# Layer 0's written order at the turn of a period: first taps, position weights, transposes and output sums

## The chip, the cores and the metric

The kernel runs on one core of one Trainium2 chip. The metric is the device time of one execution in microseconds. The core's engines are named as in the profile: PE (TensorE), with its weight loads PEld; DVE (VectorE); ACT (ScalarE); POOL (GpSimd); SP (SyncE, which here issues DMAs). Each engine works through its own list of instructions, and semaphores order the lists among each other.

## The reference, cut to what matters

The input x has the shape (2, 512, 64, 64). Two layers follow each other, each added to its input. Layer 0 is a deformable convolution on a group norm of x; layer 1 is an attention with batch norm, and the change doesn't touch it. Of layer 0:

```python
xproj = inp @ in_w + in_b                        # inp: x, normalised, channels last
x1 = depthwise_conv_3x3(x, dw_w) + dw_b
x1 = layernorm_over_channels(x1) * ln_g + ln_b
x1 = gelu(x1)
offset = x1 @ off_w + off_b                      # 16 groups, 9 points, 2 coordinates
mask = softmax((x1 @ mask_w + mask_b).reshape(N, H, W, 16, 9), -1)
out = sum over the 9 points of mask * bilinear(xproj at base + offset)
out = out @ out_w + out_b
x = x + out
```

The kernel's fast path reads the offsets as smaller than one pixel: then every output pixel is a weighted sum over a 5 x 5 window of xproj, with weights that follow from offsets and mask.

## The kernel before

Layer 0 is cut into 16 chunks (NSEQ), 8 rows of one image each. Four stages work on a chunk. Each is a Python generator whose `yield` ends a step:

- `project` (L724): three loads of raw rows; four ACT activations that write xn, the normalised rows (L748); then four times the projection pq on PE (L758), its copy xj on ACT (L764), and two stores to the padded image xt in HBM (L766).
- `features` (L771): one step of four ACT activations, the first tap of the depthwise convolution for each of four blocks of channels (L783); 32 taps on DVE (L788), eight a block, where POOL adds the blocks up (`tot`, L794 and L796); the mean over channels on PE (p_mean, L801); the subtraction (L806) and squares (L809); the variance, its root on ACT (L818) and reciprocal on DVE (L820, L821); two steps of GELU on ACT (L825).
- `weights` (L833): four times a matmul group po (L842) and its sum o (L847); exp, the one-dimensional weights and the softmax's sum; nine steps (pk, L885, and aw, L890) that sum products into aw, the 25 position weights of a pixel; one ACT copy `at` (L893) that reorders them; and four steps of four transposes p_tr on PE (L901) with a copy awT on ACT (L902).
- `sample` (L919): eight steps that spread the weights (pb on PE, L930, copied to bt by ACT, L935); eight steps, in two halves s of four blocks cb, that multiply patches of xt with bt (pa, L949, 8 products, each in two passes) and copy the result to dT on ACT (L960, four copies); in the second half each also loads the residual `res` (L941), and the last step of each half loads the next chunk's patches (`fetch`, L914, eight DMAs). Then four times the output projection py (L969) and a step with its sum (L974), statistics (L975) and store (L976), called t0 to t3 here.

The main loop runs under `tc.manual_schedule()`: each engine does its instructions in the order in which Python wrote them. That order is `period` (L998). Period i calls steps of several chunks in turn: `y`, the output half of `sample(i-1)`; `v`, the last four steps (the transposes) of `weights(i)`; `m`, `sample(i)`; `w`, `weights(i+1)`; `f`, `features(i+2)` from its DVE taps on; `g`, the first step of `features(i+3)`; `p`, `project(i+3)`; and `more`, one piece of the second image's statistics (loads xraw, L711, and bn_stats, L713), which last through periods 0 to 4. `m`, `w` and `g` are handed on as `y`, `v` and `f` of the next period. "The turn" is where one period ends and the next begins.

At the turn, the order before is, by engine (numbers count the blocks of a stage):

- PE: pa12, pq2, pa13, pq3, py0, transposes 0 to 3, pb0, pb1, po0. (pa12 is half 1, block 2.)
- ACT: GELU, xj1, dT12, xj2, dT13, first taps, xj3, `at`, awT0 to awT3, bt0, bt1.
- DVE: pk7, pk8, four taps, t0 and its statistics, nine taps, o0, seven taps, o1, and so on.
- SP: stores of xj2, load of res3, eight patch loads, stores of xj3, one xraw, three raw loads, store of t0.

In PSUM, tiles of tag "mm" (pq, py, p_tr, po, p_mean and the group norm's) share four buffers in rotation, tiles of tag "big" (pb, pa) two.

Of the kernel before, what the change touches and what calls it, by code (L numbers as in the profile page):

```python
# [570 lines left out]
def window_path(ctx: ExitStack, tc: tile.TileContext, t_in: dict, out: bass.AP, far: bass.AP, sums: bass.AP):  # L571
# [58 lines left out]
    with ExitStack() as l0:  # L630
# [66 lines left out]
        def image_stats(n):  # L697

            mv = sm.tile([P, KB, 2], F32, name="gn_mv")
            size = CH if n == 0 else CH // 2  # L700
            pieces, ahead = deque((kb, h) for kb in range(KB) for h in range(S // size)), deque()
            for kb in range(KB):
                st = sm.tile([P, 16, 6], F32, name="gn_st")
                for h in range(S // size):
                    if n == 0:
                        t = img[kb][:, h * size : (h + 1) * size]
                    else:
                        while len(ahead) < 3 and pieces:
                            k2, h2 = pieces.popleft()
                            ahead.append(io.tile([P, size], F32, name="xraw", bufs=3))  # L710
                            nc.sync.dma_start(ahead[-1], x_v[n, :, k2, h2 * size : (h2 + 1) * size])  # L711
                        t = ahead.popleft()
                    nc.vector.bn_stats(st[:, h, :], t)  # L713
                    yield
                nc.vector.bn_aggr(mv[:, kb, :], st[:, : S // size].rearrange("p a b -> p (a b)"))
            yield
            result = []
            yield from group_norm_steps(mv, KB, sm, ps, result)
            sc, bi = result
            gn[n] = [sm.tile([P, KB], F32, name=f"gn_{k}{n}") for k in ("scale", "bias")]  # L720
            nc.vector.tensor_copy(gn[n][0], sc)
            nc.vector.tensor_copy(gn[n][1], bi)
# [184 lines left out]
        def fetch(i, s):  # L907

            if i >= NSEQ:
                return  # L910
            n, ch = divmod(i, NCH)
            t = io.tile([P, PX, C], F32, name="patch", bufs=2)
            for p in range(PX):
                nc.sync.dma_start(  # L914
                    t[:SN, p, :], xt_d[n][ch * ROWS + PR * s : ch * ROWS + PR * s + SY, PC * p : PC * p + SX, :]
                )
            patches[i, s] = t

        def sample(i):  # L919

            n, ch = divmod(i, NCH)
            at = [awT[32 * t : 32 * t + NW].rearrange("w g (c s r p) -> w c r g s p", c=2, s=2, r=PR) for t in range(4)]

            for d0 in range(0, PR * PC, 4):
                pb = ps.tile([P, 4, 2 * PX * G], F32, tag="big", bufs=2, name="pb")

                for k in (0, 2, 1, 3):
                    r, c = divmod(d0 + k, PC)
                    off, t = SEL0 - (r * SX + c), c // 2
                    nc.tensor.matmul(  # L930
                        pb[:SN, k, :], sel[32 * t : 32 * t + NW, off : off + SN], at[t][:, c % 2, r], start=True, stop=True
                    )

                copy = nc.vector.tensor_copy if i == NSEQ - 1 and d0 % PC else nc.scalar.copy
                copy(bt[:SN].rearrange("s g q d -> s d (g q)")[:, d0 : d0 + 4, :], pb[:SN])  # L935
                yield
            res = {}

            def read(cb):
                res[cb] = io.tile([P, CH], F32, name="res", bufs=4)  # L940
                nc.sync.dma_start(res[cb], x_v[n, :, cb, ch * CH : (ch + 1) * CH])  # L941

            dT = cv.tile([P, KB, CH], F32, tag="dT", name="dT", bufs=2)
            for s in range(2):
                xp = patches.pop((i, s))
                for cb in range(KB):
                    pa = ps.tile([P, PX, 4, PR * PC], F32, tag="big", bufs=2, name="pa")
                    for p in range(PX):
                        nc.tensor.matmul(  # L949
                            pa[:, p], xp[:SN, p, cb * P : (cb + 1) * P],  # L950
                            bt[:SN, 4 * cb : 4 * cb + 4, PX * s + p, :], start=True, stop=True,
                        )

                    for q in range(4):
                        rows = slice(CG * q, CG * (q + 1))
                        dst = dT[rows, cb, s * (CH // 2) : (s + 1) * (CH // 2)].rearrange(
                            "p (r q c) -> p q r c", r=PR, c=PC)
                        src = pa[rows, :, q, :].rearrange("p q (r c) -> p q r c", c=PC)
                        copy = nc.vector.tensor_copy if i == NSEQ - 1 and q % 2 else nc.scalar.copy
                        copy(dst, src)  # L960
                    if s:
                        read(cb)
                    if cb == KB - 1:
                        fetch(i + 1, s)
                    yield
            for cb in range(KB):
                py = ps.tile([P, CH], F32, tag="mm", name="py")
                for kb in range(KB):
                    nc.tensor.matmul(  # L969
                        py, out_w[:, kb, cb * P : (cb + 1) * P], dT[:, kb, :], start=(kb == 0), stop=(kb == KB - 1)  # L970
                    )
                yield
                t = res.pop(cb)
                nc.vector.scalar_tensor_tensor(t, py, out_b[:, cb : cb + 1], t, ALU.add, ALU.add)  # L974
                nc.vector.bn_stats(stats2[n][:, cb, ch, :], t)  # L975
                nc.sync.dma_start(x1_d[n][ch][:, cb, :], t)  # L976
                yield
# [20 lines left out]
        def period(y, v, m, w, f, g, p, more):  # L998

            p()
            y()
            v(4)
            f(4)
            y()
            for taps in (9, 7, 6, 6):
                m(2)
                w()  # L1010
                more()
                f(taps)
                w()
                more()
            w()
            m()
            w()
            m()
            f()
            y()  # L1020
            f()
            m()
            p()
            w(2)
            y(2)
            w()
            m()
            p()
            f()
            w(2)  # L1030
            p()
            y(2)
            f()
            y()
            m()
            p()
            more()
            for k, steps in enumerate((1, 2, 2, 2)):
                p()
                w(steps)  # L1040
                if k == 0:
                    f()
                p()
                more()
                if k < 3:
                    m()
                if k == 0:
                    f()
                if k == 2:
                    g()  # L1050
            w()

        def value_weights():

# [26 lines left out]
        v = Chain(weights, 0)  # L1081
        v(23)
        run(features(1), project(2), output_bias())
        fetch(0, 0)
        fetch(0, 1)
        later, y, f = image_stats(1), Chain(sample, NSEQ), Chain(features, 2)
        with tc.manual_schedule():
            f()
            for i in range(NSEQ):
                if i == NCH - 3:  # L1090
                    run(later)
                w, m, g = Chain(weights, i + 1), Chain(sample, i), Chain(features, i + 3)
                period(y, v, m, w, f, g, Chain(project, i + 3), lambda: next(later, None))
                y, v, f = m, w, g
            y.rest()
# [5 lines left out]
    with ExitStack() as l1, tc.manual_schedule():  # L1101
# [8 lines left out]
        with ExitStack() as at, ExitStack() as inner:  # L1110
# [177 lines left out]
            for n in range(NB):  # L1288
# [9 lines left out]
                for i in range(NCH // 2):  # L1298
                    if 0 < i < 3 or n and i == 0:
                        k = i + 1 if i else 1  # L1300
# [26 lines left out]
                for qb in range(NCH):  # L1327
                    acc = {}
                    for kp in range(NPAIR + 2):
# [23 lines left out]
                        if kp < NPAIR:  # L1353
                            v = ready.pop(0)
                            e, tt, _ = made[qb, kp]
                            ops = operands(lambda k: e[:, k, :], tt)
                        else:
                            v = w7[:, kp - NPAIR]
# [174 lines left out]
```

## Time and profile before

| What | us |
|---|---|
| median of three runs | 3701.42 (3700.8 to 3702.75) |
| the profiled execution's own time | 3707.44 |
| its span, first to last instruction | 3705.6 |
| of it, layer 0's periods 1 to 5 and the end of 0 (233 to 615) | 382 |
| of it, periods 6 to 12 (615 to 1089) | 474 |
| of it, periods 13 to 15 and the last outputs (1089 to 1276) | 187 |

A period is counted from the first output projection py0. Periods 6 to 12 are 67.7 us each; periods 1 to 5, which also carry statistics of the second image, are 74.0 to 75.9 us; from chunk 13 on there is nothing left to project, and the periods are shorter. All times in microseconds "from the start" are on the clock of this one profiled execution.

In lines of instructions, the columns are start, duration, engine, line, operation, output <- inputs with shapes and the count of instructions merged into the line; in brackets stands how long the engine was idle before, and what ended it. In lines of waits: engine, what waited, <- what it waited for, then the total, the number of waits, and the longest.

### The profile page before, as it was taken

To read this page: it belongs to the slowest core of one execution; us is meant where nothing else is said; L and a number is where in the kernel's file an instruction comes from. 1 tells how busy PE (TensorE), PEld (TensorE's weight loads), DVE (VectorE), ACT (ScalarE), POOL (GpSimd) and SP (SyncE) were. 2 spreads that over 40 slices of the span, in tenths; PEclk is the share of its full clock that TensorE was granted. 3 is DMA by queue.
4 is the path that set the end of the run, shared out by engine and by line. 5 is a ranking of instruction groups with operands and counts; after the bars stand their busy time and mean duration, and the time that the engine had idled before them with its cause. 6 is when DMAs were issued, how large, how long until landed. Compare 5 with 4: busy or idle time off the path is not lost.

```text
span 3705.6 us, 39010 instructions
## 1 busy us (share of the span) xinstructions
PE 3417.9 (92%) x15151; PEld 2433.8 (66%) x15151; DVE 2345.8 (63%) x3575; ACT 1304.1 (35%) x1691; POOL 291.0 (8%) x190
## 2 busy tenths in 40 slices
PE   4689998999998799999999999999999999999990
PEld 1355555555555477777777777777777777777770
DVE  5798989999996475545554554567455455545544
ACT  2476777787886321111111111221111111111114
POOL 2112111212111030000000000022000000000000
PEclk9789999999999899999999999999999999999995
DMA  7233442342432444334334333444433333243349
GB/s 240 63 98 114 135 137 83 115 133 83 127 109 78 142 157 171 126 129 139 123 108 163 122 125 130 140 155 169 149 121 111 122 138 111 101 149 121 111 162 389
DMA packets 180181, 500.06 MB, mean 135 GB/s; under 512 B 22640, under 2 KB 64368, under 8 KB 170512
## 3 DMA queue, kind: packets, MB, share of 16 engines
q1 hardware_dynamic: 176496, 473.34, 37.5%
q10 hardware_dynamic: 3456, 24.12, 1.7%
q8 instruction: 121, 1.98, 0.2%
q14 instruction: 76, 0.62, 0.0%
q0 software_dynamic: 32, 0.00, 0.0%
HBM read 406.09 MB, written 91.29 MB: 134 GB/s over the span
## 4 chain that ended last, share of the span: by engine, by line
PE 75%; DVE 15%; DMA 4%; ACT 2%; SPq 1%; issue 1%; POOL 1%; ACTq 0%; DVEq 0%; POOLq 0%
PE acc L1364 41%; DVE conv L788 8%; PE pS L1211 7%; PE p L1402 7%; PE py L969 5%; PE pq L758 4%; PE pa L949 4%; PE pv L1251 3%; PE pk L1305 1%; PE p_mean L801 1%; DVE pk L885 1%; DVE aw L890 1%; DMA patch<-xt 1%; DMA out<-ct 1%; DVE o L847 1%
## 5 line engine op out<-in xcount | busy, mean ns | idle before, releaser
L1364 PE MATMUL acc<-e,v 128*128 128x256 f32 x3072 | 768.2, 386 | 0.0
L1215 ACT ACTIVATE e<-pS 128x1024 f32<-128x1024 f32 x256 | 262.0, 1024 | 1386.4 <-PE pS L1211 1313.0
L1364 PE MATMUL acc<-tt,v 128*128 128x256 f32 x3072 | 748.2, 380 | 0.5 <-DMA v<-wv 0.5
L1364 PEld LDWEIGHTS acc<-e,v 128*128 128x128 f32 x3072 | 566.5, 190 | 233.2 <-issue 165.3
L1364 PEld LDWEIGHTS acc<-tt,v 128*128 128x128 f32 x3072 | 582.4, 190 | 91.2 <-issue 10.6
L1218 DVE TENSOR_TENSOR t<-e 128x256 f32<-128x256 f32 x256 | 108.8, 425 | 761.1 <-ACT e L1215 761.1
L788 DVE SCALAR_TENSOR_TENSOR conv<-xn,L_conv_dw_w_sb,conv 128x504 f32<-128x504 f32 (+1 forms) x512 | 399.7, 795 | 48.5 <-ACT conv L783 36.5
L1228 DVE TENSOR_TENSOR tot<-tot,e 128x512 f32<-128x512 f32 x480 | 330.1, 688 | 8.3
L949 PEld LDWEIGHTS pa<-bt,patch 96*128 96x128 f32 x2048 | 251.8, 197 | 63.1 <-issue 39.4
L1211 PE MATMUL pS<-q,kq 64*128 64x512 f32 x1024 | 289.0, 641 | 0.0
L949 PE MATMUL pa<-bt,patch 96*128 96x128 f32 x2048 | 255.3, 281 | 9.3 <-ACT dT L960 5.8
L935 ACT COPY bt<-pb 96x1024 f32<-96x1024 f32 x124 | 234.2, 2001 | 58.9 <-PE pb L930 58.9
L758 PE MATMUL pq<-L_conv_in_w_sb,xn 128*128 128x512 f32 x512 | 236.3, 605 | 4.3 <-ACT xn L748 4.3
L969 PE MATMUL py<-dT,L_conv_out_w_sb 128*128 128x512 f32 x512 | 238.0, 610 | 0.0
L1402 PE MATMUL p<-t,v 128*128 128x256 f32 x1024 | 231.4, 382 | 1.7 <-DMA v<-wv 1.7
L1402 PEld LDWEIGHTS p<-t,v 128*128 128x128 f32 x1024 | 192.1, 190 | 48.5 <-issue 21.2
L960 ACT COPY dT<-pa 32x256 f32<-32x256 f32 x496 | 179.5, 362 | 89.8 <-PE pa L949 80.9
L842 PE MATMUL po<-om_w_pg,feat 128*128 128x432 f32 x512 | 203.4, 542 | 0.0
L969 PEld LDWEIGHTS py<-dT,L_conv_out_w_sb 128*128 128x128 f32 x512 | 99.3, 197 | 119.6 <-issue 115.5
L758 PEld LDWEIGHTS pq<-L_conv_in_w_sb,xn 128*128 128x128 f32 x512 | 94.1, 194 | 109.5 <-issue 93.0
L842 PEld LDWEIGHTS po<-om_w_pg,feat 128*128 128x128 f32 x512 | 93.0, 191 | 90.5 <-issue 89.4
L1211 PEld LDWEIGHTS pS<-q,kq 64*128 64x128 f32 x1024 | 77.1, 184 | 84.9 <-issue 84.9
(203 smaller groups left out, 3731.2 us busy)
## 6 DMA issues: line engine op xcount, KB each, us to landing
v<-wv SPq DMA_DIRECT2D x252, 768.0 KB
patch<-xt SPq DMA_DIRECT2D x256, 192.0 KB
v<-wv SPq DMA_DIRECT2D x256, 128.0 KB
wv<-v SPq DMA_DIRECT2D x32, 896.0 KB
xt<-xj SPq DMA_DIRECT2D x128, 128.0 KB
res<-in_x SPq DMA_DIRECT2D x64, 256.0 KB
wx<-res SPq DMA_DIRECT2D x64, 256.0 KB
xq<-wx SPq DMA_DIRECT2D x16, 1024.0 KB
```

The lines of the kernel that those rows point to most:

```text
L758: nc.tensor.matmul(pq, xn[:, kb, 1 + 2 * t : 3 + 2 * t, :].rearrange("p r c -> p (r c)"), in_w[:, kb, :], start=(kb == 0), stop=(kb == KB ...
L788: nc.vector.scalar_tensor_tensor(dst, src, wt, dst, ALU.mult, ALU.add)
L842: nc.tensor.matmul(po[:, : 3 * GP], f[:, kb, t * P : (t + 1) * P], om_w[:, kb].rearrange("p a k g -> p (a k g)"), start=(kb == 0), stop=(k ...
L935: copy(bt[:SN].rearrange("s g q d -> s d (g q)")[:, d0 : d0 + 4, :], pb[:SN])
L949: nc.tensor.matmul(pa[:, p], xp[:SN, p, cb * P : (cb + 1) * P], bt[:SN, 4 * cb : 4 * cb + 4, PX * s + p, :], start=True, stop=True,)
L960: copy(dst, src)
L969: nc.tensor.matmul(py, out_w[:, kb, cb * P : (cb + 1) * P], dT[:, kb, :], start=(kb == 0), stop=(kb == KB - 1))
L1211: nc.tensor.matmul(pS[:, h, :], kq[r, 2 * (kp // 4) + h, c0 : c0 + P], qs[qb][r, :], start=True, stop=True)
L1215: nc.scalar.activation(e.rearrange("p a q -> p (a q)"), pS.rearrange("p h q -> p (h q)"), AF.Exp)
L1228: nc.vector.tensor_add(tots[qb], tots[qb], e2[:, h, :])
L1364: nc.tensor.matmul(acc[j][:, cb * HQ : (cb + 1) * HQ], v[:, j, cb * P : (cb + 1) * P], ops[j], start=(kp + cb == 0), stop=(kp + cb == NPAI ...
L1402: nc.tensor.matmul(p7[:, cb * HQ : (cb + 1) * HQ], v7[:, cb * P : (cb + 1) * P], t3, start=(k + cb == 0), stop=(k + cb == NPAIR + 2),)
```

## The change

`period` is written anew around the turn, and `sample` gets one more `yield`, between the products pa and their copies to dT, so that the two can be called apart. Everywhere but in the last of the eight such steps `m(2)` calls them together, as `m()` did.

By engine, the turn then reads (what moves is in bold):

- PE: pa12, pq2, pa13, pq3, **transposes 0 to 3, py0**, pb0, pb1, po0.
- ACT: GELU, **first taps**, xj1, dT12, xj2, **`at`**, xj3, **dT13**, awT0 to awT3, bt0, bt1.
- DVE: as before: pk7, pk8, four taps, t0 and its statistics, nine taps, o0.
- SP: stores of xj2, **stores of xj3, one xraw**, load of res3, eight patch loads, three raw loads, store of t0.

No instruction is added or taken away.

```diff
@@ sample
                             bt[:SN, 4 * cb : 4 * cb + 4, PX * s + p, :], start=True, stop=True,
                         )
+                    yield
 
                     for q in range(4):
@@ period
             p()
+            v(4)
             y()
-            v(4)
             f(4)
             y()
             for taps in (9, 7, 6, 6):
@@
             w()
-            m()
+            m(2)
             w()
-            m()
+            m(2)
             f()
             y()
             f()
-            m()
+            m(2)
             p()
             w(2)
             y(2)
             w()
-            m()
+            m(2)
             p()
             f()
             w(2)
@@
             y(2)
             f()
             y()
+            m(2)
+            p()
+            more()
+            p()
+            w()
+            f()
+            p()
+            more()
+            m(2)
+            f()
+            p()
+            w(2)
+            g()
+            p()
+            more()
+            m(2)
+            p()
+            w(2)
+            p()
+            more()
             m()
             p()
+            w(3)
+            p()
             more()
-            for k, steps in enumerate((1, 2, 2, 2)):
-                p()
-                w(steps)
-                if k == 0:
-                    f()
-                p()
-                more()
-                if k < 3:
-                    m()
-                if k == 0:
-                    f()
-                if k == 2:
-                    g()
-            w()
+            m()
```

## The prediction

> **What bounds the kernel now.** I read the page first, then a table of busy time by stretches, then the chain of waits inside one stretch, then the waits of single engines there, and last each engine's instructions in order of time around one turn.
>
> The page gives shares of the whole span, which mixes layer 0 (to about 1270 us) with the attention layer:
>
> ```profile
> PE 3417.9 (92%) x15151; PEld 2433.8 (66%) x15151; DVE 2345.8 (63%) x3575; ACT 1304.1 (35%) x1691; POOL 291.0 (8%) x190
> ```
>
> The change touches layer 0's main loop alone, so I cut that loop at the output projection (py, L969) that opens each period. The stretches show start:end, length, and the busy time of PE, PEld, DVE, ACT and POOL:
>
> ```profile
> 750.64:818.34 67.70, 64.44 (x310) 38.34 (x309) 62.67 (x72) 53.77 (x73) 12.98 (x9) 1.00 0.36 113
> 818.34:886.04 67.70, 64.45 (x310) 38.34 (x309) 62.69 (x72) 53.76 (x73) 12.99 (x9) 1.00 0.37 113
> ```
>
> A period takes 67.70 us, and both PE (64.4) and DVE (62.7) are nearly full. Neither can lose time without lengthening the loop, unless the loss lies in the 3.3 us (PE) or 5.0 us (DVE) they have left. The chain of waits from 750.64 says which engine has its turn on the path:
>
> ```profile
> 750.64 3.45 PE py L969 x8
> 754.09 0.03 issue
> 754.12 0.76 DVE res L974
> ...
> 780.06 1.28 POOL tot L796
> ...
> 781.38 1.12 PE p_mean L801 x2
> ...
> 814.91 3.44 PE pq L758 x8
> 818.34 0.43 PE py L969
> ```
>
> So the loop is a ring of two halves. From the output sum t0 (754.12, DVE L974) DVE sets the time: it holds the other 28 convolution taps, which end at 779.95; POOL adds the last one; the mean (p_mean) starts at 781.38. That is 27.26 us. From the mean to the next t0 PE sets the time, matmul upon matmul: 781.38 to 821.82, 40.44 us. 27.26 + 40.44 = 67.70.
>
> What is idle in the ring, over 682.94 to 953.75 (four turns), first DVE, then PE:
>
> ```profile
> DVE conv L788 <- ACT conv L783: 7.3, 4, 1.8
> DVE res L974 <- PE py L969: 5.7, 4, 1.4
> ```
>
> ```profile
> PE p_mean L801 <- POOL tot L796: 4.9, 4, 1.3
> PE p_tr L901 <- ACT at L893: 4.4, 4, 1.1
> PE pb L930 <- ACT awT L902: 3.3, 4, 0.8
> ```
>
> At each turn DVE waits 1.8 us for the first tap from ACT and 1.4 us for py; PE waits 1.1 us for the copy `at` before the transposes and 0.8 us for awT after them. These waits the change addresses. Here is ACT at that turn:
>
> ```profile
> 812.12 1.48 ACT L960 COPY dT<-pa 32x256 f32<-32x256 f32 x4
> 813.63 0.58 ACT L764 COPY xj<-pq 128x512 f32<-128x512 f32 x1
> 814.94 1.49 ACT L960 COPY dT<-pa 32x256 f32<-32x256 f32 x4 [0.73 <-PE pa L949]
> 816.46 2.93 ACT L783 ACTIVATE conv<-xn,L_conv_dw_b_sb,L_conv_dw_w_sb 128x512 f32<-128x512 f32 x4
> 819.41 0.58 ACT L764 COPY xj<-pq 128x512 f32<-128x512 f32 x1
> 819.89 2.93 ACT L893 COPY at<-aw 128x1600 f32<-128x1600 f32 x1
> ```
>
> [...] at all turns the written order is the order run, and t0 waits 1.42 us with 28 ready taps behind it. [...] after 4.99 us of idle p_mean took 2.08 us, after 1.25 us it took 1.12.
>
> **The change part by part**, on the turn at 818.34. Up to pq3 PE's order is the same, so PE's times to 818.34 stand.
>
> (a) First taps (L783, 2.93 us) go ahead of xj1, dT12, xj2 on ACT, right behind GELU (ends 811.62, from 809.07 + 2.55). They end at 814.57, before DVE's last sum pk8 (814.73 + 0.76 = 815.49). DVE's wait of 1.82 is gone: four taps run 815.5 to 818.6.
>
> (b) `at` goes ahead of xj3 and of the last copies dT13. ACT's row then reads: taps to 814.57, xj1 0.5, dT12 1.5, xj2 0.5, so free at 817.06 (1.6 us after pk8, the backlog of the taps); `at` 817.06 to 820.0 (2.93); xj3 to 820.5; dT13 to 822.0; awT0 to 822.6 (0.59 us each, 0.49 apart).
>
> (c) Transposes go ahead of py0. They start at 820.05, not 822.88, and take 1.97 us. But pq3 ends at 818.34, and py0, which filled PE between 818.2 and 821.8, now stands behind them. py0 needs dT13 (822.0) and its PSUM buffer: tag "mm" has four, and four tiles before py0 is now the first p_tr, read by awT0 (822.6). So py0 runs 822.65 to 826.25 and t0 starts at 822.65 + 3.64 (what lay between 818.18 and 821.82) = 826.29: **4.47 us later than 821.82**. DVE, done with the four taps at 818.6, idles 7.7 us where it idled 3.24; 28 taps are queued behind t0, and the mean waits for them. Without the buffer, dT13 or the transposes' end alone give 822.0: 3.9 us. Both ends say a loss.
>
> (d) After py0 PE goes straight on (pb at 826.1, before 825.67: only 0.4 later), so PE isn't what is late: o0 needs po0 at t0 + 8.2, and po0 ends at t0 + 4.
>
> (e) What is late next: PE is done with pa01 0.43 us later, but the mean 4.47 later, so PE's wait before p_mean grows from 1.24 to about 5.3 us. At such waits its clock is down. In periods 1 to 5, which carry the second image's statistics, the wait is already 5.87, 7.26, 5.74, 4.99 and 6.67 us, and from p_mean's start to the next pa it takes 7.42, 6.61, 6.98, 5.82 and 7.46 us, against 4.40 (781.38 to 785.78): 3.0, 2.2, 2.6, 1.4, 3.1 more. This is on the path, as rstd (797.42) meets DVE without slack (797.45), and the GELU and everything of (b) follow it. 5.3 us lies at the short end of that row: I take 2.0, ends 0 and 3.1. Periods 6 to 12 are new to it, 7 x 2.0 = 14; period 13 has 0.9 us of slack there (rstd at 1134.99, DVE free at 1135.86): 1.1.
>
> (f) Turns that differ. At turn 5 the group norm of image 1 already delays DVE; by the same sums ACT's gn_var, now behind dT13, ends 543.9 (was 544.45), awT0 544.3, t0 at 548.0 (was 547.97): nothing. At turns 14 and 15 no projection and no taps are left and `at` waits for DVE's sums (1153.96 and 1210.89, unchanged); py0 filled that wait and now follows the transposes (end 1159.36 and 1217.5), cold. I take 7 us for a cold py0 (twice 3.6) and subtract what pb and po no longer lose to the cold clock (0.9 + 1.5; 0.9 + little): 3.5 and 5, together 8.5, ends 3 and 12.
>
> (g) SP: at the turn the xraw load and xj3's stores now stand ahead of dT13's res3 and its 8 patch loads (5.65 us on SP), where the load stood behind them. Second statistics after t0 wait 1.62, 2.87, 2.05 and 1.34 us for xraw at turns 1 to 4 (issue 6.56 us after t0, landed 4.2 later). With SP free about 5.1 us after the later t0, each gains up to 1.46: minus 5 in all, ends 0 and minus 8. Patch and raw loads start later, with over 25 us until their use. POOL's memset follows `at`, earlier. The yield at L953 adds no instruction.
>
> **Sum.** 4.47 us at turns 1 to 4 and 6 to 13: 12 x 4.47 = 53.6; clock 14 + 1.1; late turns 8.5; loads minus 5: +72.2. Profiled run 3707.44 (span 3705.6) becomes 3779.6. It lies 6.0 above the median of the runs shown, and nothing in the sum depends on that, so on the median: 3701.42 + 72.2 = 3774.
>
> **Rivals.**
> 1. The clock stays up[...]: 53.6 - 5 + 6 = +55, 3756. For it: 5.3 is at the edge of what was seen. Against it: all five waits from 4.99 us began cold.
> 2. Cold at the turn too: wait 1.7, transposes 1.97, wait 0.6 make 4.3 us without large matmuls, and py0 starts cold, up to 2.4 us more on 12 turns: 3774 + 29 = 3803. Against it: today's 1.1 + 1.97 + 0.83 = 3.9 us leave pb warm (1.14 us) in every steady turn.
> 3. The loss stays PE's 0.43 us a turn, +5 to 3707, because DVE makes up the rest. Against it: DVE's 62.67 us busy, 1.8 of small gaps and 7.7 of wait make 72.2, more than 67.70.
> 4. Faster: t0 isn't late, because py0 keeps its place in time. It decides where py0 starts no later than pq3's end (818.34); then only the loads' waits go, 7.9 us: 3693. It would take matmuls out of written order, or that the change doesn't place them as read; no turn of the trace shows either.
>
> **How the numbers follow.** The forecast has 0.65, rivals 1 to 4 have 0.19, 0.11, 0.02, 0.03. The low end takes 3.9 us a turn and little clock (12 x 3.9 - 5 + 3 = 45), the high end 3.1 us of clock, 12 late and part of rival 2: 3746 to 3798. A difference under 0.2% (7 us) can't be told from none here: faster 0.03, same 0.02, slower 0.95.
>
> **What would show it.** Right: periods of 72 to 75 us from turn 6; DVE's wait for the first taps gone, its wait for py about 7.7 us; PE's wait before p_mean about 5.3 us and p_mean at 2.08; p_tr ahead of py. Wrong: a t0 no later than 3.7 us after pq3's end, or taps that run while t0 waits.

## The result and the profile after

The changed kernel takes 3792.77 us (median of four, 3790.77 to 3797.85), the kernel before 3701.85: a ratio of 1.0248, with a 95% interval of 1.023 to 1.0266. The profiled execution took 3792.37 us, its span is 3790.6, so it is 85.0 us above the span of before. Layer 0's last output projection ends at 1360.0 us instead of 1276.0: 84 of the 85 us are in layer 0.

The page's line of busy times, and the stretches of two periods, here cut at the first transpose, as py no longer opens the turn:

```profile
PE 3446.8 (91%) x15151; PEld 2444.0 (64%) x15151; DVE 2342.9 (62%) x3575; ACT 1301.8 (34%) x1691; POOL 290.8 (8%) x190
```

```profile
789.46:864.50 75.04, 67.66 (x309) 39.31 (x309) 62.57 (x71) 53.55 (x73) 12.96 (x9) 0.95 0.35 102
864.50:939.60 75.10, 67.65 (x309) 39.29 (x309) 62.58 (x71) 53.57 (x73) 12.98 (x9) 0.95 0.34 102
```

A period is 7.4 us longer than the 67.70 of before. DVE's work is the same (62.6); PE's is 3.2 us longer with the same instructions, at a mean clock of 0.95 instead of 1.00. So about 3 us are a slower PE, and the rest is waiting. Where, say DVE's waits and then PE's, over four turns (714 to 1015 us):

```profile
DVE res L975 <- PE py L970: 31.0, 4, 7.8
DVE rstd L820 <- ACT rstd L818: 12.0, 4, 3.0
```

```profile
PE p_mean L801 <- POOL tot L796: 20.9, 4, 5.2
PE p_tr L901 <- ACT at L893: 8.7, 5, 1.7
PE py L970 <- ACT awT L902: 1.8, 4, 0.5
```

DVE no longer waits for the first taps (1.8 us before), but 7.75 us for py, where it was 1.4. PE's wait before p_mean is 5.2 us (1.2 before), and the reciprocal of the deviation now waits for ACT (0 before), because PE gave the variance late: from p_mean to the mean of the squares it takes 14.38 us (897.91 to 912.29), where it takes 11.41 before and as much in e5_warm_pe below (747.14 to 758.55), with the clock at 1.00. The chain of waits through the turn at 864.50 shows what py0 waited for:

```profile
864.25 0.62 ACT xj L764
864.87 0.25 ACT dT L961
...
866.27 0.60 ACT awT L902
866.87 0.04 issue
866.91 3.71 PE py L970 x8
870.63 0.02 issue
870.65 0.76 DVE res L975
```

Before, py0 followed pq3 without a gap and nothing of ACT stood on the chain here. Now the chain runs over ACT: xj3, dT13, awT0, then py0, then t0. The three engines at this turn, ACT, PE, DVE:

```profile
856.08 2.93 ACT L783 ACTIVATE conv<-xn,L_conv_dw_b_sb,L_conv_dw_w_sb 128x512 f32<-128x512 f32 x4
859.03 0.59 ACT L764 COPY xj<-pq 128x512 f32<-128x512 f32 x1
...
861.50 2.94 ACT L893 COPY at<-aw 128x1600 f32<-128x1600 f32 x1
864.25 0.62 ACT L764 COPY xj<-pq 128x512 f32<-128x512 f32 x1
864.77 1.48 ACT L961 COPY dT<-pa 32x256 f32<-32x256 f32 x4
866.27 2.05 ACT L902 COPY awT<-p_tr 128x512 f32<-128x512 f32 x4
```

```profile
859.17 3.60 PE L758 MATMUL pq<-L_conv_in_w_sb,xn 128*128 128x512 f32 x8
864.50 1.97 PE L901 MATMUL p_tr<-ident,at 128*128 128x128 f32 x16 [1.72 <-ACT at L893]
866.91 3.70 PE L970 MATMUL py<-dT,L_conv_out_w_sb 128*128 128x512 f32 x8 [0.45 <-ACT awT L902]
...
897.91 2.07 PE L801 MATMUL p_mean<-tot,ones_c 128*128 128x512 f32 x2 [5.22 <-POOL tot L796]
899.78 5.66 PE L970 MATMUL py<-dT,L_conv_out_w_sb 128*128 128x512 f32 x8
```

```profile
859.84 3.08 DVE L788 SCALAR_TENSOR_TENSOR conv<-xn,L_conv_dw_w_sb,conv 128x504 f32<-128x504 f32 x4
870.65 0.75 DVE L975 SCALAR_TENSOR_TENSOR res<-py,L_conv_out_b_sb,res 128x512 f32<-128x512 f32 x1 [7.73 <-PE py L970]
```

The four taps are done at 862.9, t0 starts at 870.65. From pq3's start to t0 it is 870.65 - 859.17 = 11.48 us; before it was 821.82 - 814.74 = 7.08:

```profile
814.74 3.60 PE L758 MATMUL pq<-L_conv_in_w_sb,xn 128*128 128x512 f32 x8
818.18 3.60 PE L969 MATMUL py<-dT,L_conv_out_w_sb 128*128 128x512 f32 x8
822.88 1.97 PE L901 MATMUL p_tr<-ident,at 128*128 128x128 f32 x16 [1.10 <-ACT at L893]
```

```profile
821.82 0.75 DVE L974 SCALAR_TENSOR_TENSOR res<-py,L_conv_out_b_sb,res 128x512 f32<-128x512 f32 x1 [1.42 <-PE py L969]
```

The turn costs 4.40 us: PE waits 1.72 us for `at`, the transposes take 1.97, and PE waits 0.45 us more for py0's buffer. Counted from pq3's start, py0 starts 4.30 us later than before, and it runs 0.10 us longer. After the 5.22 us of wait, p_mean takes 2.07 us for 1.12, and py1 5.66 for 3.60.

### The profile page after: what moved, and what is told of

The parts are those of the page before. It is cut to its first block, busy times and chain, and to the rows that moved or that the text cites. A ratio compares the mean times of both kernels' runs of the same rounds, so it can differ in the third digit from the quotient of the medians.

```text
span 3790.6 us, 38949 instructions
## 1 busy us (share of the span) xinstructions
PE 3446.8 (91%) x15151; PEld 2444.0 (64%) x15151; DVE 2342.9 (62%) x3575; ACT 1301.8 (34%) x1691; POOL 290.8 (8%) x190
## 4 chain that ended last, share of the span: by engine, by line
PE 77%; DVE 13%; DMA 4%; ACT 2%; issue 2%; SPq 1%; POOL 1%; ACTq 0%; DVEq 0%; POOLq 0%
PE acc L1374 41%; DVE conv L788 8%; PE pS L1221 7%; PE p L1412 6%; PE py L970 6%; PE pq L758 5%; PE pa L949 4%; PE pv L1261 4%; PE pk L1315 2%; PE p_mean L801 1%; DMA xraw<-in_x 1%; DMA out<-ct 1%; DVE o L847 1%; DMA patch<-xt 1%; DMA L_conv_in_w_sb<-in_L_conv_in_w 1%
## 5 line engine op out<-in xcount | busy, mean ns | idle before, releaser
L1374 PEld LDWEIGHTS acc<-tt,v 128*128 128x128 f32 x3072 | 582.4, 190 | 91.7 <-issue 10.6
L949 PEld LDWEIGHTS pa<-bt,patch 96*128 96x128 f32 x2048 | 251.4, 197 | 61.7 <-issue 36.8
L970 PE MATMUL py<-dT,L_conv_out_w_sb 128*128 128x512 f32 x512 | 256.7, 649 | 7.4 <-ACT awT L902 7.4
L801 PE MATMUL p_mean<-tot,ones_c 128*128 128x512 f32 x32 | 32.1, 1106 | 119.8 <-POOL tot L796 119.8
```

The source lines that it names most:

```text
L949: nc.tensor.matmul(pa[:, p], xp[:SN, p, cb * P : (cb + 1) * P], bt[:SN, 4 * cb : 4 * cb + 4, PX * s + p, :], start=True, stop=True,)
L970: nc.tensor.matmul(py, out_w[:, kb, cb * P : (cb + 1) * P], dT[:, kb, :], start=(kb == 0), stop=(kb == KB - 1))
L1374: nc.tensor.matmul(acc[j][:, cb * HQ : (cb + 1) * HQ], v[:, j, cb * P : (cb + 1) * P], ops[j], start=(kp + cb == 0), stop=(kp + cb == NPAI ...
```

## The experiments

Ratios are to runs of the kernel before on the same chip, whose medians there were 3702.8 (e1 to e4), 3704.6 (e5 to e8) and 3703.6 us (e9, e10). Steady periods are periods 6 to 12, which carry no statistics of the second image. A cold or low clock is PE's clock granted as 0.50 in the traces; otherwise it is at 1.00.

| Run | us | ratio, 95% interval | steady period, us |
|---|---|---|---|
| e1_py_first | 3747.56 | 1.0112 (1.0095 to 1.0129) | 69.0 or 70.6 |
| e2_dt_first | 3800.08 | 1.0255 (1.0238 to 1.0273) | 76.0 or 77.6, mean 76.8 |
| e3_taps_first | 3722.17 | 1.0042 (1.0025 to 1.0059) | 67.7 or 69.3 |
| e4_late_t0 | 3702.62 | 0.9996 (0.9987 to 1.0005) | 66.7 |
| e5_warm_pe | 3771.48 | 1.0178 (1.0161 to 1.0195) | 72.2 |
| e6_taps_late_t0 | 3684.60 | 0.9947 (0.9931 to 0.9964) | 65.5 |
| e7_deep_xraw | 3780.19 | 1.0204 (1.0187 to 1.0221) | 75.1 |
| e8_taps_late_t0_deep | 3656.97 | 0.9873 (0.9857 to 0.9889) | 65.5 |
| e9_before_deep | 3691.98 | 0.9969 (0.9957 to 0.9980) | as before |
| e10_late_t0_deep | 3677.22 | 0.9929 (0.9913 to 0.9946) | 66.7 |

### Does py0 behind the transposes make the loss, or dT13 behind `at`?

```diff
 # e1_py_first, against the changed kernel
             p()
-            v(4)
             y()
+            v(4)
             f(4)
```

> The changed kernel, with py0 written ahead of the transposes again; the first taps ahead and the copies dT13 behind `at` stay. Theory (py0 waits for the last of transposes, dT13 and the buffer that awT0 frees): py0 now waits for dT13 alone, 3.9 us after its old place, so t0 is about 3.9 us later than in the kernel before; PE's wait before p_mean is then about 2.5 us, its clock stays up, periods 6 to 12 are 71.6 us, the time is about 3759 us. Rival (the transposes ahead of py0 are the whole loss): periods 67.7 us and about 3702 us.

It took 3747.56 us. The rival falls: without the transposes in front, steady periods are still 1.2 us or more over 67.7. But the theory had the wrong size for dT13. PE's instructions at a turn of this run:

```profile
706.58 2.74 PE L970 MATMUL py<-dT,L_conv_out_w_sb 128*128 128x512 f32 x6
710.32 1.13 PE L970 MATMUL py<-dT,L_conv_out_w_sb 128*128 128x512 f32 x2 [1.00 <-ACT dT L961]
```

Six of py0's eight passes, those of the first three blocks, run while dT13 is still being copied; the last two alone wait, 1.0 us. From p_mean (669.78) to the next t0 (711.49) it is 41.71 us, 1.27 more than before and not 3.9. So in the changed kernel it isn't py0's own wait for dT13 that holds it: the wait for `at`, the transposes and the PSUM buffer hold it from its first pass. dT13 has a part in the last of these alone, as awT0 stands behind it on ACT, and that wait is 0.45 us.

Nor is dT13 most of the 45 us that this run loses. In periods 1 to 4 it takes 35.7 to 37.4 us from t0 to p_mean, where the kernel before takes 31.0 to 33.3: 18 us in sum. Here DVE waits 36.8 us for xraw over 240 to 560 us, as in e3_taps_first below.

A second surprise: PE's wait before p_mean was 2.5 us, as expected, and the clock fell all the same in some periods. One of them:

```profile
738.74 1.12 PE L801 MATMUL p_mean<-tot,ones_c 128*128 128x512 f32 x2 [2.53 <-POOL tot L796]
739.70 5.29 PE L970 MATMUL py<-dT,L_conv_out_w_sb 128*128 128x512 f32 x8
```

p_mean itself ran at full speed, and py1 behind it slowly (3.60 in the period before): the granted clock was 0.98 in the mean from 737 to 740 us and 0.50 from 740 to 743 us. These are the periods of 70.6 us among those of 69.0.

```diff
 # e2_dt_first, against the changed kernel
-            m()
+            m(2)
             p()
             w(3)
             p()
             more()
-            m()
```

> The changed kernel, with the last copies dT13 ahead of `at` again; the transposes stay ahead of py0. Theory: `at` ends 1.5 us later, the transposes at 823.5 on the clock of the period before, t0 is about 5.3 us late, PE's clock is down at p_mean, periods of 75.9 us, 3798 us. Rival (moving dT13 is the loss): periods 67.7 us, 3702 us.

3800.08 us for 3798; the rival falls. DVE's wait for py is 10.6 us a turn (42.5 over four), PE waits 3.2 us for `at`, 1.5 more than in the changed kernel, and p_mean comes after 5.2 us of wait at 2.08 us. So moving dT13 behind `at` spared 1.5 us of wait. But the sum fits better than its parts. At the turns PE's clock is down as well: the transposes take 3.42 or 3.68 us for 1.97, and at every other turn py0 takes 4.7 for 3.7, which makes the periods 0.9 us longer than forecast. Against that, from t0 to p_mean periods 1 to 4 take 29.5 to 30.4 us, where the changed kernel takes 31.8 to 33.1.

### Do the first taps, moved alone, cost anything?

```diff
 # e3_taps_first, against the kernel before
                 p()
                 w(steps)
                 if k == 0:
                     f()
+                if k == 1:
+                    g()
...
-                if k == 2:
-                    g()
```

> The kernel before with one part of the change alone: the first taps right behind GELU. Theory: DVE's wait for them (1.8 us) goes, but t0 still waits for py0, so DVE's wait for py grows by as much; dT13 is 0.4 us later: periods 67.7 to 68.1 us, 3702 to 3712 us. Rival (the taps' delay of xj, dT and `at` on ACT is what the change loses by): periods above 70 us, over 3730 us.

3722.17 us, outside both: 10 us over the theory's end, 8 under the rival's. The steady turn is as expected: DVE's wait for py is 3.33 us, which is the old 1.4 and 1.8 together, and four of seven steady periods are 67.7 us. The other three are about 1.5 us longer, by the clock, granted here as 0.57 in the mean from 728 to 731 us and as 0.86 from 731 to 734 us:

```profile
728.35 2.02 PE L801 MATMUL p_mean<-tot,ones_c 128*128 128x512 f32 x2 [2.05 <-POOL tot L796]
```

The rest is in periods 1 to 4. There DVE's waits for xraw, over 240 to 560 us, come to 31.9 us, where the kernel before has 7.9:

```profile
DVE gn_st L713 <- DMA xraw<-in_x: 31.9, 12, 3.6
```

So this part of the change gains nothing at the turn and makes loads late that no theory had counted.

### Is it the taps queued behind t0?

```diff
 # e4_late_t0, against the changed kernel
-            f(4)
+            f(13)
             y()
-            for taps in (9, 7, 6, 6):
+            for taps in (5, 5, 5, 4):
```

> The changed kernel with t0 written behind 13 taps where it is behind 4; PE's and ACT's orders are the changed ones. Theory (the loss is taps queued on DVE behind a late t0, and the clock that falls in the wait it makes): DVE's wait for py shrinks from 7.7 to under 1 us, p_mean comes when PE is there, periods near 67 us, 3670 to 3690 us, below the kernel before. Rival (PE's order or ACT's backlog is the loss in itself): periods stay above 72 us, time above 3760 us.

3702.62 us: 90 us under the changed kernel with PE's and ACT's orders untouched. The rival falls. t0 is as late as ever, but DVE has taps to do meanwhile; its waits over five turns:

```profile
DVE rstd L820 <- ACT rstd L818: 7.0, 5, 1.4
DVE res L975 <- PE py L970: 4.4, 5, 0.9
```

Periods are 66.7 us: PE's wait before p_mean is gone, and its clock stays up (p_mean takes 1.02 us, 2.07 in the changed kernel). That is 1.0 us under the kernel before. Yet the time was to be 3670 to 3690 us: periods 1 to 4 took 75.6 to 77.7 us (before: 74.0 to 75.9), with waits for xraw and a cold clock (p_mean at 2.07 or 2.08 us after waits of 6.3 to 7.7 us), and gave back what the others won (e10_late_t0_deep below shows that the waits for xraw did it).

### How much is PE's clock?

```diff
 # e5_warm_pe, against the changed kernel
-            def mean_over_c(tot):
+            def mean_over_c(tot, extra=0):
                 p = ps.tile([P, CH], F32, tag="mm", name="p_mean")
+                for _ in range(extra):
+                    nc.tensor.matmul(p, ones, out_w[:, 0, :], start=True, stop=True)
                 nc.tensor.matmul(p, ones, tot, start=True, stop=True)
...
-            mu = mean_over_c(tot)
+            mu = mean_over_c(tot, 5)
```

> The changed kernel with five more matmuls (ones by out_w, into the p_mean tile, overwritten by the mean's own) ahead of each mean, about 4.3 us of work in PE's wait of 5.2 us; nothing that is computed changes. Theory (the second part of the loss, 2.9 us a period, is PE's clock falling in that wait): p_mean at 1.12 us instead of 2.08, periods 6 to 12 of 72.1 instead of 75.05 us, about 3771 us. Rival (what follows p_mean is late for another reason): no change, 3792 us, or later by the added work.

3771.48 us: five matmuls of no use ahead of each mean make the kernel 21 us faster. A mean and a period of this run:

```profile
747.14 1.13 PE L803 MATMUL p_mean<-tot,ones_c 128*128 128x512 f32 x2 [0.88 <-POOL tot L796]
```

```profile
747.14:819.32 72.18, 68.99 (x319) 39.98 (x319) 62.63 (x72) 53.63 (x73) 13.00 (x9) 1.00 0.36 106
```

The clock is at 1.00, p_mean at 1.13 us, and the period at 72.18: 75.09 less 2.9. What stays, 72.2 - 67.7 = 4.5, is the late t0. The two parts are thereby apart.

### What makes periods 1 to 4 longer still?

```diff
 # e7_deep_xraw, against the changed kernel (e8, e9 and e10 have the same two lines)
-                        while len(ahead) < 3 and pieces:
+                        while len(ahead) < 5 and pieces:
                             k2, h2 = pieces.popleft()
-                            ahead.append(io.tile([P, size], F32, name="xraw", bufs=3))
+                            ahead.append(io.tile([P, size], F32, name="xraw", bufs=5))
```

> The changed kernel with xraw loaded five pieces ahead in five buffers instead of three in three. Theory (the extra loss in periods 1 to 4 is statistics on DVE that wait for loads which stand on SP behind the stores of a later xj1): DVE no longer waits for xraw, t0 to p_mean in these periods falls from 31.8 to 33.1 us to about 29.7, together 12 us less: 3780 us. Rival (these waits are hidden by the wait for py): 3792 us.

3780.19 us. From t0 to p_mean, periods 1 to 4 now take 30.2, 30.3, 29.5 and 29.5 us, and DVE's waits for xraw are gone from them. The mechanism can be read in the changed kernel, around the turn at 402 us, on ACT, SP and DVE:

```profile
393.36 2.93 ACT L783 ACTIVATE conv<-xn,L_conv_dw_b_sb,L_conv_dw_w_sb 128x512 f32<-128x512 f32 x4
396.31 0.59 ACT L764 COPY xj<-pq 128x512 f32<-128x512 f32 x1
```

```profile
396.93 1.09 SPq L766 DMA_DIRECT2D xt<-xj  x2
398.12 0.53 SPq L711 DMA_DIRECT2D xraw<-in_x  x1
```

```profile
400.60 0.43 DVE L713 BATCH_NORM_STATS2 gn_st<-xraw 128x6 f32<-128x256 f32 x1 [2.47 <-DMA xraw<-in_x]
```

xj1 stands behind the first taps on ACT, its stores stand on SP until xj1 is there (396.9), the load of xraw stands behind those stores (398.1), and the statistics on DVE wait 2.47 us for it. In the changed kernel this wait is hidden, as t0 is later still (DVE's wait for py is 3.9 us in these periods, not 7.7); in e3_taps_first nothing hides it. The wait that counts in the changed kernel is behind t0: 2.40, 2.73, 3.44 and 2.16 us at turns 1 to 4, where the kernel before has 1.62, 2.87, 2.05 and 1.34. At turn 3 that load is issued at 413.65, 5.7 us after t0 (before: 401.61, 7.3 after it), and its statistics start 7.1 us later (before: 4.2). SP's patch loads end 2.9 us after t0 there, and 1.2 us after it before; that they slow the load is likely, but no run shows it apart.

### Versions that beat both kernels

```diff
 # e6_taps_late_t0, against e3_taps_first
-            f(4)
+            f(9)
             y()
-            for taps in (9, 7, 6, 6):
+            for taps in (7, 6, 5, 5):
```

> The kernel before with the first taps right behind GELU and t0 behind 9 taps instead of 4 (the other groups then 7, 6, 5, 5): PE's order is that of the kernel before. Theory: DVE's waits at the turn (1.8 and 1.4 us) both go, p_mean comes when PE is there, periods 6 to 12 of about 65.8 us (PE's busy time is 64.4), periods 1 to 4 stay near 75 us for the xraw loads: about 3687 us. Rival (DVE's order at the turn is not what sets the period): 67.7 us or more, 3702 us or more.

3684.60 us, and periods of 65.5 us. With the taps early and t0 late, both of DVE's waits at the turn are gone, and PE's wait before p_mean too (p_mean takes 1.02 us). PE keeps the old order, with py0 in the wait for `at`.

> As e6_taps_late_t0, with xraw loaded five ahead. Theory: periods 1 to 4 lose their waits for xraw too and are about 70 us: about 3662 us, below both kernels. Rival (loads five ahead collide with patch and raw loads, or the wait isn't on the path): as e6_taps_late_t0.

This is e6_taps_late_t0 with the two lines of e7_deep_xraw. It is the fastest, 3656.97 us. A period of it:

```profile
652.73:718.25 65.52, 64.23 (x309) 38.24 (x309) 62.26 (x72) 53.98 (x72) 12.62 (x9) 1.00 0.37 118
```

PE is busy for 64.2 of 65.5 us. What is left are its waits of 0.8 us for awT and 0.4 us for `at`.

> The kernel before with xraw loaded five ahead and nothing else. Theory: only its own waits for xraw in periods 1 to 4 (0.8 + 1.6 + 2.9 + 2.1 + 1.3 us) go: about 3693 us; the deeper loads alone don't give what e8_taps_late_t0_deep gives (3657 us). Rival (the loads' depth is most of that gain): 3675 us or less.

e9_before_deep has those two lines in the kernel before, alone: 3691.98 us, 12 us better. So the loads' depth alone is the smaller part of the 48 us that e8_taps_late_t0_deep gains, and worth more there (28 us over e6_taps_late_t0) than alone. With deeper loads in both kernels (e7_deep_xraw against this run, each taken against its own runs of the kernel before) the change costs 87 us instead of 91: the loads of xraw are a small part of its loss.

> The changed kernel with t0 behind 13 taps (e4_late_t0) and xraw five ahead. Theory (what kept e4_late_t0 at 3702 us with periods of 66.7 us are its waits for xraw in periods 1 to 4, 4 to 6.5 us each, and the clock that falls with them): periods 1 to 4 of about 69 us, 3675 us. Rival (something else in the changed order holds periods 1 to 4): 3695 us or more.

e10_late_t0_deep has them in e4_late_t0: 3677.22 us, with periods 1 to 4 of 68 to 72 us. So it was the waits for xraw that held e4_late_t0 at 3702 us. It stays 20 us behind e8_taps_late_t0_deep, with periods of 66.7 against 65.5, which is 8 of the 20: the turn with py0 behind the transposes is the worse one even where DVE waits less than 1 us for py, as PE then waits 1.8 us for `at` with nothing to do and 0.4 us for awT (0.4 and 0.8 there).

## Why the prediction was right, point by point

The mechanism and its size at the turn were right, and 3792.77 us lies in the range of 3746 to 3798, but near its upper end: the middle of the forecast, 3774 us, is 19 us short. The table finds 13 of these in the terms beside the turn. The other 6 lie between traces and medians: the traced run of the kernel before is 5.6 us above the median of its runs, that of the changed kernel 0.4 below, and where in the kernel these 6 us lie no run shows. Of the sum, in microseconds of the profiled spans:

| Term | forecast | measured |
|---|---|---|
| t0 later at turns 1 to 4 and 6 to 13 | 53.6 (4.47 each) | 52.9 (4.41 each) |
| clock, periods 6 to 12 | 14 (2.0 each) | 20.6 (2.9 each) |
| clock, periods 1 to 5 (already slow before) | 0 | -0.7 |
| turn 5 | 0 | 1.6 |
| loads of xraw, periods 1 to 4 | -5 | 2.8 |
| before turn 1 | 0 | 1.1 |
| period 13's clock and turns 14, 15 | 9.6 | 5.6 |
| after layer 0 | 0 | 1.0 |
| sum | 72.2 | 84.9 |

The measured terms come from differences between the two traces. From p_mean to the next t0 it takes 40.4 us before, 47.7 to 47.8 after in periods 6 to 12; of this, 2.85 us and a little more lie between p_mean and py2, which is the clock, and 4.41 behind it. From t0 to p_mean nothing changed in periods 5 to 12 (27.27 before, 27.25 after at period 6), and in periods 1 to 4 it is 2.8 us longer in sum. The 1.1 us before turn 1 aren't the change's: the changed kernel's trace is 1.3 us behind at the very first mean already (79.44 against 78.13 us), and over all twelve traces that mean comes anywhere from 76.1 to 81.9 us.

- **(a) and (b)** held: DVE's wait for the first taps is gone, ACT's backlog puts `at` 1.6 us behind the end of pk8 (861.50 against 859.92), and xj3, dT13 and awT0 follow as counted.
- **(c)** held in its main number, 4.41 for 4.47, and in DVE's wait, 7.74 for 7.7. Two small errors cancel in it: the buffer held py0 for 0.45 us where 0.63 was forecast, and py0 ran 0.1 us longer. Its aside was wrong: dT13 alone costs 1.3 us, not 3.9 (e1_py_first), because only the last quarter of py0 reads it.
- **(e)** held in kind and was too small: 2.9 us a period for 2.0. I took the short end of five measured costs since the wait was among the shorter ones; the cost came out near the long end, in every period. e5_warm_pe shows by itself that this much is the clock. I let the cost follow the length of the wait; in the traces it goes with the time at the low clock, 6.83 us here (last section). In the five periods that I took it from, the clock was low for 10.24, 6.83, 6.83, 3.41 and 10.24 us, for costs of 3.0, 2.2, 2.6, 1.4 and 3.1 us.
- **(f)** turn 5 wasn't free: awT0 ended when expected, but py0, after 2.06 us of wait, ran in 5.40 us instead of 3.6, with the clock at 0.50 from 566.01 to 569.42 us. At turns 14 and 15 py0 took 4.06 and 3.65 us, not the 7 that I took for a cold one: it followed 3.7 us of transposes, and the clock was back at 1.00 from 0.93 and 0.09 us after its start.
- **(g)** had the wrong sign. It looked at the loads behind t0, which SP was to reach sooner, and counted only the moves on SP itself. The load behind t0 was issued about when counted (5.7 us after t0 for 5.1), but its statistics started 7.1 us later instead of 4.2 (both at turn 3). These waits sum to 10.73 us for 7.88, which is the 2.8 us of the table. The later patch loads were counted as harmless, by their own use alone; whether they did it stays open. It also missed that the first taps, moved on ACT, delay xj1, whose stores SP waits for, with an xraw load behind them; the late t0 hides this here, and e3_taps_first shows it bare. e7_deep_xraw shows that all waits for xraw together cost 12 us, those of the kernel before among them.
- **Rival 1**, a clock that stays up, fell: the 13 means of periods 1 to 13 came at 2.07 or 2.08 us. **Rival 2**, a clock already down at py0, appears at turn 5 alone (and at the steady turns of e2_dt_first); in the other turns with taps py0 took 3.70 us. **Rivals 3 and 4** fell with the 4.41 us a turn.

## What to carry to other kernels

On DVE, 28 taps that waited for nothing stood behind t0 here, which waited for PE; none ran ahead of it, and its wait of 7.7 us was paid in full. Moving such an instruction back by as much work as the wait is long comes before making the producer faster: in e4_late_t0, nine taps of 0.76 us ahead of that wait won 90 us, and nothing but five numbers changed. A step that fills another engine's wait has to be counted as removed cover when it is moved: py0's 3.60 us stood in PE's wait for `at` and left 1.10 us of it, and with py0 moved 1.72 us were open. And of every step moved on a compute engine, follow what the DMA queue waits for from it: here a late xj1 made its stores late, and with them the xraw load queued behind, for which DVE waited 2.47 us at the turn at 402 us.

## What the runs showed of the hardware that was not expected

PE's clock fell after waits as short as 2.05 us (e3_taps_first) and 2.53 us (e1_py_first), in some periods and not in others of the same kernel. In e3_taps_first, after waits of 2.00 to 2.08 us, p_mean took 2.02 or 2.07 us in three of the periods 6 to 12 and 1.12 or 1.13 us in the other four. In the slow periods of e1_py_first p_mean still ran at full speed or near it (1.12 to 1.25 us), and py1 was slow (5.29 us for 3.60 at 739.70).

In the clock records of both kernels' traces the clock is at 0.50 or 1.00, and it changes only at edges that stand whole multiples of 3.41 us apart; the shortest time at one clock is 3.413 us. In e3_taps_first it is low from 728.44 to 731.85 us. In the 3.41 us before that, from 725.03 us on, PE was busy for 1.36 us: the whole wait of 2.05 us lies in them. In the next period the wait is as long (2.07 us, before the mean at 797.74), but 796.71 us, which is 20 times 3.413 us after 728.44, cuts it. PE is busy for 2.38 and 2.39 us of the 3.41 us before and after that time, and the mean takes 1.13 us. So of two waits of one length, the one that lies whole between two such times was followed by a low clock, with PE busy for 1.36 of the 3.41 us, and the one cut in two was not. That this is what decides is a reading of these two cases; no run moved a wait alone.

The cost of a fall goes with the time at the low clock. In e3_taps_first the 3.41 us at the low clock are all worked through; at a clock of 0.50 half of them, 1.7 us, is lost by this estimate, and the slow periods are 1.4 to 1.7 us longer. In the changed kernel the clock is low for 6.83 us, as from 897.10 to 903.93 us; PE still waits in the first 0.81 us, and half of the other 6.0 is 3.0 us. From p_mean's start to the next pa it takes 7.37 us there and 4.40 in the kernel before: 2.97 were measured.

In the changed kernel and in e7_deep_xraw the periods settle at one length, 75.05 to 75.11 us from period 8 on, and the clock's cost with it. That is 22 times 3.413 us, and the clock records agree: in the changed kernel the clock falls at 746.92, 822.01, 897.10, 972.20 and so on to 1197.47 us, each time 75.09 or 75.10 us after the last. In e2_dt_first, periods of 77.6 and 76.0 us take turns, and two of them make 153.6 us, 45 times 3.413. So in these runs the loop's length, or that of two rounds of it, is a whole multiple of 3.413 us; what pulls it there, no run tested.
